# A diffusion-transformer block with a routed MLP on one core: queries turned by VectorE and exchanged through DRAM, in another order of steps

## The chip, the core and the metric

The kernel runs on one core of one Trainium2 chip. The metric is the device time of one execution in microseconds (us), the median of three runs. All operands that matter here are float32, and all sizes below are per execution.

## What is computed

The reference, cut to the part around the change (16 sequences of 256 tokens, width 256, 16 heads of 64):

```python
shift = jax.nn.silu(t) @ W_ada.T + b_ada
h = _ln(x, ln1_g, ln1_b) + shift
qkv = (h @ Wqkv.T).reshape(b, n, 3, H, HD)
q = _ln(qkv[:, :, 0].transpose(0, 2, 1, 3), qn_g, qn_b)   # per head, over its 64 values
k = _ln(qkv[:, :, 1].transpose(0, 2, 1, 3), kn_g, kn_b)
v = qkv[:, :, 2].transpose(0, 2, 1, 3)
scores = jnp.einsum('bhnd,bhmd->bhnm', q, k) / jnp.sqrt(jnp.float32(HD))
attn = jax.nn.softmax(scores, axis=-1)
o = jnp.einsum('bhnm,bhmd->bhnd', attn, v)
x = x + o.transpose(0, 2, 1, 3).reshape(b, n, H * HD) @ Wout.T
```

Behind it come a gate over 8 experts, the choice of the 512 best tokens of each expert, a norm, a two-layer MLP per expert (256 to 1024 to 256, GELU) on the chosen tokens, and an addition of the weighted results to the tokens.

## The kernel before

The kernel has two phases. The first does, sequence by sequence, the norm, the projections to queries, keys and values, the attention, the output projection and the gate logits. The second chooses tokens and runs the experts, in 16 jobs (8 experts, two halves of their tokens); the change touches it only in the buffers of a few small tiles.

**One sequence in the first phase.** `First` normalises 256 tokens and turns them on TensorE (L646). `Group` (L671) stands for 512 of the 3072 projected columns and 128 tokens: there are twelve in a sequence, with g = 0, 1 for queries, 2, 3 for keys, 4, 5 for values, and t = 0, 1 for the two halves of the tokens. Each runs two matmuls of 128x512 (L683). Query and key groups are then squared on ScalarE (L696), summed per head on VectorE (L700), raised to -0.5 on GpSimd (L103) and scaled on VectorE (L716). A head's 64 values now lie along the free dimension and have to lie along the partitions.

**Two ways to turn them.** Queries go through TensorE: four transposes of 128x128 (L725), and ScalarE reads the result from PSUM, applies the gain and bias of the norm and writes it to `qT` (`evict`, L737). Keys of sequences 1 to 14 go another way. VectorE transposes them in blocks of 32x32 (`turn`, L749). When both halves of a group pair are done, SP writes the 512 KB to a DRAM tile (`away`, L756, one DMA) and reads them back with the blocks in their places (`back`, L764, four DMAs of 32 partitions and 128 KB each). ScalarE then applies gain and bias in place (`affine`, L770). The attention probabilities take the same way: VectorE turns them (`turn`, L832), SP writes them away (L840) and brings them back (L854), eight times a sequence. One write with its four reads is called an exchange below. Sequences 0 and 15 (`DIRECT`) use no exchange at all.

**Attention.** `Quad` handles four heads, in two steps of two: scores (L794), maxima on VectorE (L802), exponentials with sums on ScalarE (L811), reciprocal on VectorE (L818), normalising on GpSimd (L822), the turn and its exchange, and the product with the values (L881). `Tail` is the output projection (L907), the residual (L914), a second norm, two stores of 128 KB, and the gate logits (L944).

**What sets the order.** Nothing is scheduled at run time. Each step is entered in a `Plan` with an engine, a duration and the buffers it uses, and a table `PLACES` holds one number for each step. The program is the steps sorted by that number (L1497), and each engine runs its instructions in that order. The steps of several sequences are thus interleaved by hand. All DMAs of the first phase stand on SP's queue in this order too; an SP instruction that waits holds up all behind it. Buffers are rings: three 512 KB tiles `pb` hold what VectorE turned, keys and probabilities alike; four DRAM tiles `blocks`; four tiles `prT` for what came back; two of `qT`, `kT`. The entries in the plan for an exchange read

```python
at(q + 10, "SP", 0.36, partial(a.away, i), [pb], [(1, blocks)], [pb, blocks], lag=1.0)
at(q + 11, "DMA", 1.6, nothing, [(1, blocks)], [blocks], [pb], lag=1.7)
at(q + 14, "SP", 1.6, partial(a.back, i), [blocks], [(1, prT)], [blocks, prT], lag=0.0)
at(q + 15, "DMA", 2.6, nothing, [(1, prT)], [prT], [blocks], lag=1.7)
```

so that the plan gives the transfers of an exchange 1.6 + 2.6. The "DMA" steps issue nothing. Loads of `x` and the stores of `Tail` have no "DMA" step.

Of the kernel before, what the change touches and what calls it, by code (L numbers as in the profile page):

```python
# [9 lines left out]
F32 = mybir.dt.float32  # L10
I32 = mybir.dt.int32
BF16 = mybir.dt.bfloat16
AF = mybir.ActivationFunctionType
# [5 lines left out]
P = 128  # L19
B, N, D = 16, 256, 256  # L20
# [44 lines left out]
def kernel(  # L65
# [83 lines left out]
    def make_others():  # L149
# [33 lines left out]
        0, 0, 3.3, 4.54, 3.75, 5.04, 4.42, 7.33, 0.23, 0, 8, 9.39, 18.02, 16.03, 11.2, 13.11,  # L183
        23.2, 20.01, 0, 0, 0, 0, 0, 0, 0, 4.02, 4.97, 5.83, 3.5, 4.21, 6.16, 6.67, 7.33, 10.88,
        12.83, 14.5, 15.29, 17.42, 23.39, 24.13, 14.6, 16.55, 19.41, 20.2, 22.6, 25.38, 26.05,
        12.61, 14.56, 15.43, 17.17, 22, 22.79, 23.46, 18.21, 20.16, 21.4, 22.19, 24.59, 25.83,
        26.72, 29.9, 32.28, 31.78, 34.69, 26.28, 28.23, 28.97, 30.46, 32.44, 39.3, 40.4, 33.51,
        35.46, 36.17, 37.06, 39.25, 44.82, 45.92, 35.24, 37.19, 37.9, 38.94, 41.05, 47.16, 47.98,
        40.04, 42.03, 42.74, 43.53, 45.51, 49.93, 50.64, 42.21, 46.59, 48.2, 50.15, 28.01, 30.17,
        31.32, 33.31, 36.97, 37.69, 29.57, 30.36, 34.22, 41.77, 43.49, 33.04, 45.27, 29.03, 31.7,  # L190
        32.77, 35.24, 44.38, 45.43, 30.77, 33.73, 36.15, 43.94, 44.94, 34.97, 46.29, 47.38, 37.41,
        38.65, 39.44, 46.32, 56.74, 58.42, 41.65, 42.53, 45.41, 58.91, 60.37, 43.77, 63.58, 38.43,
        39.85, 41.07, 47.23, 62.1, 62.91, 40.45, 43.98, 48.14, 62.69, 63.4, 45.22, 64.6, 67.15,
        53.84, 55.37, 58.91, 60.42, 69.53, 70.25, 56.57, 57.46, 61.33, 72.14, 72.9, 60.15, 78.82,
        61.08, 62.32, 63.89, 66.36, 71.7, 72.41, 62.92, 64.85, 67.27, 72.58, 73.39, 66.09, 79.84,
        80.93, 76.93, 82.47, 83.26, 84.77, 90.28, 91.04, 78.53, 79.32, 85.68, 93.62, 97.65, 84.5,
        98.81, 77.95, 80.33, 84.22, 87.6, 89.84, 90.55, 79.13, 85.18, 86.69, 94.06, 96.49, 86.42,
        97.79, 100.1, 113.62, 117.31, 119.21, 119.11, 120.6, 121.31, 132.34, 133.24, 134.29,
        135.07, 124.06, 129.13, 130.78, 130.28, 131.14, 131.65, 134.74, 135.18, 136.69, 137.38, 0,
        25.19, 25.9, 27.27, 12.59, 13.3, 15.1, 47.76, 48.65, 50.38, 52.33, 53.04, 53.83, 55.97,  # L200
        63.13, 65.81, 54.86, 56.96, 57.67, 58.46, 60.44, 61.64, 52.11, 54.06, 54.77, 55.71, 58.27,
        65.47, 66.48, 57.18, 59.87, 61.04, 62.24, 64.22, 65.01, 65.81, 67.17, 70.47, 72.07, 76.37,
        59.35, 61.3, 69.97, 71.92, 66.07, 68.02, 68.73, 69.52, 71.5, 74.75, 75.47, 67.8, 69.75,
        70.46, 71.4, 73.38, 74.17, 73.02, 74.97, 75.68, 76.47, 79.73, 81.3, 82.47, 75.2, 77.22,
        77.93, 78.72, 80.93, 81.86, 82.66, 84.02, 87.32, 88.92, 93.22, 81.75, 86.64, 88.11, 90.06,
        85.21, 86.59, 87.38, 92.27, 93.76, 87.79, 88.84, 93.18, 94.37, 90.08, 95.17, 96.53, 99.83,
        101.43, 108.83, 90.72, 91.96, 94.57, 98.56, 100.76, 93.16, 95.53, 97.65, 100.15, 96.77,
        101.56, 104.03, 107.33, 109.11, 117.09, 119.02, 96.77, 99.55, 100.59, 103.75, 105.35,
        98.35, 99.14, 102.84, 104.14, 102.57, 106.15, 107.51, 110.95, 117.51, 127.68, 99.68,
        101.97, 103.18, 107.74, 109.6, 101.37, 102.22, 106.83, 108.99, 106.56, 110.59, 114.31,  # L210
        117.61, 121.71, 128.7, 132.26, 103.03, 105.96, 106.99, 111.44, 112.79, 104.75, 105.54,
        110.53, 112.18, 108.53, 113.59, 115.91, 119.71, 124.31, 139.03, 105.93, 107.33, 108.12,
        112.35, 115.81, 107.93, 109.58, 113.26, 114.6, 112.01, 116.61, 120.11, 123.41, 126.91,
        140.05, 143.4, 110.87, 113.4, 114.33, 118.2, 119.82, 114, 115.29, 117.29, 119.21, 117.02,
        128.61, 132.71, 136.01, 141.21, 147.73, 109.85, 111.41, 117.1, 121.61, 123.7, 115.21,
        118.06, 120.7, 124.31, 120.43, 125.11, 131.11, 134.41, 137.01, 146.71, 148.82, 161.94,
        165.79, 166.94, 166.94, 167.8, 171.31, 179.5, 180.6, 181.82, 182.8, 173.1, 177.15, 180.31,
        179.07, 180.05, 180.81, 181.6, 182.35, 184, 184.96, 0, 25.71, 26.66, 27.6, 28.45, 29.7,
        31.37, 80.71, 81.52, 83.48, 86.14, 87.19, 88.51, 90.49, 94.5, 96.98, 86.23, 88.34, 89.05,
        90.39, 92.56, 95.58, 91.74, 94.07, 94.98, 95.77, 97.75, 100.7, 101.55, 94.95, 98.14,  # L220
        98.95, 99.74, 102.74, 103.53, 104.33, 105.69, 108.99, 111.71, 116.25, 104.05, 106.5,
        111.74, 113.84, 101.3, 104.14, 106.73, 108.65, 110.81, 118.11, 119.51, 106.95, 109.08,
        110.21, 114.17, 116.42, 118.31, 120.44, 122.39, 123.1, 124.4, 126.72, 129.57, 130.64,
        118.71, 120.66, 121.37, 122.52, 124.92, 127.32, 128.12, 129.51, 132.81, 134.41, 138.71,
        130.61, 132.75, 140.92, 143.89, 123.19, 125.52, 126.31, 131.95, 133.42, 126.12, 127.27,
        131.04, 132.81, 130.13, 137.61, 139.61, 142.91, 145.41, 159.19, 122.17, 127.93, 128.72,
        133.77, 136.77, 128.53, 129.68, 132.86, 136.16, 130.92, 141.31, 143.81, 147.11, 149.61,
        158.17, 161.1, 137.14, 138.47, 139.56, 142.34, 143.4, 139.07, 140.52, 143.25, 144.79,
        142.07, 145.59, 148.01, 151.31, 153.81, 172.23, 138.16, 140.27, 141.48, 144.89, 147.11,
        140.87, 142.44, 145.8, 148.32, 144.62, 149.12, 152.21, 155.51, 158.01, 171.21, 175.48,  # L230
        148.6, 149.84, 150.63, 153.77, 154.83, 150.44, 152.26, 154.68, 155.74, 153.5, 157.11,
        160.61, 169.71, 172.31, 188.93, 149.62, 151.64, 153.71, 159.02, 160.19, 152.24, 154.67,
        159.93, 162, 156.95, 162.8, 164.81, 168.11, 169.71, 187.91, 190.02, 157.3, 158.39, 159.18,
        162.88, 163.96, 158.99, 160.14, 163.79, 165.18, 162.61, 165.98, 167.34, 182.91, 185.51,
        196.77, 156.28, 159.59, 161.59, 165.61, 168.74, 161.4, 162.55, 164.7, 168.13, 163.79,
        171.81, 174.91, 178.21, 179.81, 197.79, 198.88, 207.36, 211.52, 212.87, 212.67, 213.53,
        214.04, 227.17, 227.9, 229.12, 230.2, 218.67, 222.51, 224.16, 224.13, 224.99, 229.46,
        226.8, 228.2, 231.3, 232.08, 0, 26.23, 27.42, 48.75, 27.93, 28.94, 48.42, 130.17, 131.31,
        132.56, 134.51, 135.23, 136.26, 139.67, 144.53, 145.25, 134.96, 136.91, 137.87, 138.66,
        141.47, 144.01, 142.8, 144.75, 145.46, 146.71, 148.93, 150.49, 151.59, 144.98, 146.93,  # L240
        147.72, 148.59, 151.04, 152.84, 153.64, 156.41, 159.71, 162.21, 166.75, 151.09, 153.22,
        160.06, 163.51, 152.82, 155.63, 156.35, 157.14, 160.8, 165.41, 166.08, 154.55, 156.5,
        157.21, 160.84, 162.82, 164.57, 167.59, 169.54, 170.25, 171.04, 173.85, 176.72, 177.39,
        165.86, 170.04, 172.05, 172.92, 174.97, 175.76, 176.61, 177.97, 181.31, 182.91, 187.21,
        179.87, 181.86, 184.45, 186.4, 170.34, 171.45, 172.6, 175.07, 176.37, 172.65, 173.56,
        175.98, 178.15, 174.8, 184.51, 188.11, 191.41, 194.37, 205.47, 169.32, 170.85, 171.64,
        178.16, 181.58, 173.25, 174.52, 177.25, 182.19, 176.98, 189.81, 191.17, 194.47, 196.97,
        204.45, 206.56, 177.61, 179.45, 180.9, 183.23, 184.35, 178.85, 179.64, 184.14, 185.29,
        182.96, 190.17, 192.77, 198.88, 201.17, 215.91, 178.63, 180.98, 183.61, 189.36, 194.7,
        180.38, 182.65, 186.57, 195.31, 185.12, 196.11, 199.57, 202.87, 205.37, 214.89, 217,  # L250
        189.8, 191.04, 193.89, 199.56, 201.54, 191.64, 192.43, 196.77, 200.32, 195.92, 202.34,
        207.97, 211.27, 213.77, 235.21, 194.88, 196.12, 196.91, 206.32, 207.38, 197.92, 202.57,
        207.23, 208.59, 203.81, 209.39, 212.17, 215.47, 217.07, 236.23, 237.32, 195.9, 198.52,
        201.11, 202.62, 217.22, 199.12, 200.15, 203.53, 216.61, 202.35, 218.02, 219.67, 226.26,
# [1361 lines left out]
```

## Time and profile before

| what | value |
|---|---|
| median of three runs | 1104.54 us (1104.27 to 1107.28) |
| the profiled execution | 1106.04 us, of which its span is 1104.2 us |
| granted TensorE clock, mean | 0.99 |
| exchange phase, first write of keys to last read of probabilities | 69.0 to 761.8 us |
| output projections, first to last matmul | 117.1 to 818.0 us |
| busy, whole span: PE, DVE, ACT, POOL | 1070.6, 778.9, 596.1, 616.2 us |
| DMA of SP's queue (q1) | 139520 packets, 197.71 MB |

PE is TensorE, PEld its weight loads, DVE is VectorE, ACT ScalarE, POOL GpSimd, SP the engine that issues DMAs. The profile's views used below are: the page with its busy shares and its 40 slices; the groups of instructions by line, with their busy time, mean duration of one and what ended the idle time before them; the timeline; the waits; and tables of windows, which give for a stretch of time (us from the start of the span) each engine's busy time, the granted clock, the mean busy share of the 16 DMA engines (packets that overlap are counted double, so it can exceed 1) and the GB/s moved.

### The profile page before, as it was taken

How to read it: one execution, taken by the hardware profiler on the slowest of the kernel's cores; microseconds unless marked ns; L12 is line 12 of the kernel's file. 1: busy time of each engine (PE TensorE's matmuls, PEld its weight loads, DVE VectorE, ACT ScalarE, POOL GpSimd, SP SyncE). 2: the span in 40 equal slices, each digit the busy share in tenths (PEclk: the TensorE clock that was granted, in tenths of full speed). 3: DMA queues.
4: the chain of work that ended last, by engine and by line, in shares of the span. 5: the costliest groups of instructions: out<-in, count | busy, mean ns of one | idle time of the engine just before them, and what ended most of it. 6: DMA issues, size and time to landing. Idle time of an engine off the chain costs nothing. (4 is left out here: it accounts for less than half of the span.)

```text
span 1104.2 us, 18872 instructions
## 1 busy us (share of the span) xinstructions
PE 1070.6 (97%) x5835; PEld 714.8 (65%) x5835; DVE 778.9 (71%) x2201; ACT 596.1 (54%) x1656; POOL 616.2 (56%) x997
## 2 busy tenths in 40 slices
PE   7999999999999999999899999999988999999996
PEld 4555656566565655656465655656767888888885
DVE  6657888777778777786678787676568488654540
ACT  2768666565766566566557667576522333322331
POOL 3766776776676665675657666565411233333332
PEclk9999999999999999999999999999999999999998
DMA  6013998785888787796787778895130456555661
GB/s 211 1 39 123 277 259 237 230 255 166 248 260 227 226 246 234 201 260 211 211 251 227 228 224 240 243 256 179 63 102 20 113 189 200 170 162 175 196 201 19
DMA packets 147539, 209.20 MB, mean 189 GB/s; under 512 B 15088, under 2 KB 122864, under 8 KB 147440
## 3 DMA queue, kind: packets, MB, share of 16 engines
q1 hardware_dynamic: 139520, 197.71, 60.0%
q0 software_dynamic: 6144, 8.39, 4.1%
q10 hardware_dynamic: 1776, 1.90, 0.5%
q8 instruction: 47, 0.77, 0.3%
q14 instruction: 52, 0.43, 0.1%
HBM read 121.96 MB, written 85.98 MB: 188 GB/s over the span
## 5 line engine op out<-in xcount | busy, mean ns | idle before, releaser
L683 PE MATMUL pm<-wq,hT 128*128 128x512 f32 x768 | 360.4, 605 | 5.0 <-DVE qk L716 2.8
L822 POOL TENSOR_SCALAR pr<-pr,sums 128x256 f32<-128x256 f32 x512 | 237.1, 481 | 112.2 <-DVE sums L818 92.9
L811 ACT ACTIVATE pr<-sc,nmax 128x256 f32<-128x256 f32 x512 | 238.0, 480 | 97.5 <-DVE nmax L802 80.3
L683 PEld LDWEIGHTS pm<-wq,hT 128*128 128x128 f32 x768 | 137.3, 192 | 146.1 <-issue 131.1
L103 POOL TENSOR_TENSOR ss<-ss,neghalf 128x8 f32<-128x8 f32 x128 | 210.5, 1645 | 10.6
L802 DVE TENSOR_REDUCE nmax<-sc 128x2 f32<-128x512 f32 x256 | 165.3, 676 | 16.9 <-PE sc L794 16.3
L832 DVE STREAM_TRANSPOSE pb<-pr 128x512 f32<-128x512 f32 x224 | 149.9, 690 | 18.5 <-POOL pr L822 13.6
L794 PE MATMUL sc<-kT,qT 64*128 64x256 f32 x1024 | 135.4, 397 | 0.0
L881 PE MATMUL po<-prT,v 128*64 128x256 f32 x1024 | 127.6, 388 | 1.1 <-DVE gates L950 1.1
L700 DVE TENSOR_REDUCE ss<-sq 128x8 f32<-128x512 f32 x128 | 86.0, 672 | 47.3 <-ACT sq L696 46.8
L794 PEld LDWEIGHTS sc<-kT,qT 64*128 64x128 f32 x1024 | 92.8, 188 | 40.8 <-issue 25.4
L696 ACT ACTIVATE sq<-pm 128x512 f32<-128x512 f32 x128 | 76.9, 603 | 77.3 <-PE pm L683 75.9
L1301 POOL DMA_INDIRECT out<-y,idx x32 | 51.2, 1601 | 119.8 <-DVE y L1295 66.9
L1268 PE MATMUL ph<-xT,w 128*128 128x256 f32 x512 | 117.6, 383 | 0.0
L907 PE MATMUL pw<-wo,oT 128*128 128x256 f32 x512 | 116.6, 381 | 0.3 <-DVE qk L716 0.3
L1284 PE MATMUL py<-w,hid 128*128 128x256 f32 x512 | 116.3, 380 | 0.0
L716 DVE TENSOR_TENSOR qk<-pm,ss 128x512 f32<-128x512 f32 x128 | 87.0, 681 | 36.9 <-POOL ss L103 35.9
L907 PEld LDWEIGHTS pw<-wo,oT 128*128 128x128 f32 x512 | 96.0, 190 | 23.2 <-issue 9.4
L811 ACT ACTIVATION_READ_ACCUMULATOR pr<-sc,nmax 128x1 f32 x512 | 107.6, 210 | 0.0
L881 PEld LDWEIGHTS po<-prT,v 128*64 128x64 f32 x1024 | 67.1, 137 | 61.5 <-issue 21.1
L1275 ACT ACTIVATE hid<-ph,vec 128x256 f32<-128x256 f32 x128 | 60.4, 474 | 84.2 <-PE ph L1268 76.3
L1284 PEld LDWEIGHTS py<-w,hid 128*128 128x128 f32 x512 | 95.6, 190 | 12.8
(140 smaller groups left out, 1132.6 us busy)
## 6 DMA issues: line engine op xcount, KB each, us to landing
blocks<-pb SPq DMA_DIRECT2D x112, 512.0 KB
prT<-blocks SPq DMA_DIRECT2D x448, 128.0 KB
w<-in_fc2T SPq DMA_DIRECT2D x16, 1024.0 KB
w<-in_fc1T SPq DMA_DIRECT2D x16, 1024.0 KB
kblocks<-kb SPq DMA_DIRECT2D x28, 512.0 KB
kT<-kblocks SPq DMA_DIRECT2D x112, 128.0 KB
out<-tok SPq DMA_DIRECT2D x32, 128.0 KB
xn_dram<-tn SPq DMA_DIRECT2D x32, 128.0 KB
```

The costliest lines, as they stand in the source:

```text
L103: nc.gpsimd.tensor_tensor(dst, src, neghalf[:, : src.shape[1]], ALU.pow)
L683: nc.tensor.matmul(self.pm, hTs[self.b][:, c, bass.ts(self.t, P)], wq[:, c, bass.ts(self.g, GW)], start=(c == 0), stop=(c == DC - 1),)
L716: engine.tensor_tensor(self.qk.rearrange("p (h d) -> p h d", d=HD), src.rearrange("p (h d) -> p h d", d=HD), self.ss[:, 1, :].unsqueeze(2) ...
L794: nc.tensor.matmul(self.sc[i, j][:, t, :], qTs[self.b][rows, hp, bass.ts(t, P)], keys[rows, hp] if direct else keys[rows, hp // 4, hp % 4] ...
L802: nc.vector.tensor_reduce(self.nmax[i, j], self.sc[i, j], AX.X, ALU.max, negate=True)
L811: nc.scalar.activation(self.pr[i, j][:, t, :], self.sc[i, j][:, t, :], AF.Exp, bias=self.nmax[i, j][:, t : t + 1], scale=1.0, accum_out=se ...
L822: nc.gpsimd.tensor_scalar(self.pr[i, j][:, t, :], self.pr[i, j][:, t, :], self.sums[i][:, 1, j, t : t + 1], 1.0, ALU.mult, ALU.mult,)
L832: nc.vector.transpose(self.pb[i][:, :, :, j].rearrange("p k c t n -> p t k c n"), self.pr[i, j].rearrange("p t (k c m) -> p t k c m", c=TB ...
L881: nc.tensor.matmul(self.po[j * HD : (j + 1) * HD, i, :], vs[self.b][:, c, bass.ts(4 * self.d + 2 * i + j, HD)], prT[:, j, c] if self.b in ...
L907: nc.tensor.matmul(self.pw, oTs[self.b][:, hp // 2, self.t, hp % 2, :], wo[:, hp, :], start=(hp == 0), stop=(hp == HP - 1),)
L1268: nc.tensor.matmul(self.ph[f], self.w1[:, c, bass.ts(f, P)], self.xT[:, c, :], start=(c == 0), stop=(c == DC - 1),)
L1284: nc.tensor.matmul(self.py[i], self.hid[:, f, bass.ts(i, P)], self.w2[:, f, :], start=(f == 0), stop=(f == FC - 1),)
```

## The change

Queries of sequences 1 to 14 take the keys' way: `turn` on VectorE, one write and four reads through DRAM, then gain and bias on ScalarE from a tile `qraw` (two buffers) into `qT`, in two instructions of 128x512. The four TensorE transposes and the reading of PSUM of those groups go. Routing's tiles for masks, places and choices lie in the `pb` ring in place of tiles of their own. The plan's durations of an exchange become 1.2 + 2.0 with longer lags, and all of `PLACES` is new (3863 numbers in place of 3779). In it the last output projection, which has the place 800.67 before, has the place 777.79.

```diff
             def back(self):
-                kT = self.keys()[:, self.g - 2].rearrange("p k t h m -> p k (t h m)")
+                if self.g < 2:
+                    self.raw = work.tile([P, QB, TB, HP // 2, SQ], F32, tag="qraw", bufs=2, name="qraw")
+                else:
+                    self.raw = self.keys()[:, self.g - 2]
+                raw = self.raw.rearrange("p k t h m -> p k (t h m)")
                 for q in range(QB):
                     nc.sync.dma_start(
-                        kT[bass.ts(q, SQ)], self.blocks[:, :, q].rearrange("k d n -> d k n")
+                        raw[bass.ts(q, SQ)], self.blocks[:, :, q].rearrange("k d n -> d k n")
                     )
             def affine(self):
+                if self.g < 2:
+                    qT = of_sequence(qTs, self.b, "qT", [P, HP, N])
+                    for t in range(TB):
+                        nc.scalar.activation(
+                            qT[:, 4 * self.g : 4 * self.g + 4, bass.ts(t, P)].rearrange(
+                                "p h (k m) -> p k h m", m=SQ
+                            ),
+                            self.raw[:, :, t], AF.Identity, bias=qgb[:, 1:2], scale=qgb[:, 0:1],
+                        )
+                    return
...
-                self.mask = route.tile([P, 2, 2 * P], F32, tag="mask", name="mask")
+                both = work.tile([P, 4, 2 * P], F32, tag="pb", bufs=3, name="both")
+                self.mask, self.place_ = both[:, :2], both[:, 2:]
...
-                self.places = route.tile([P, 2 * P], F32, tag="places", name="places")
+                three = work.tile([P, 3, 2 * P], F32, tag="pb", bufs=3, name="three")
+                self.places, one, self.chosen = (three[:, k] for k in range(3))
...
-                    if g > 1 and b not in DIRECT:
+                    if b not in DIRECT:
...
-                            at(p + 7, "DMA", 1.6, nothing, [(1, blocks)], [blocks], [kb], lag=1.7)
+                            at(p + 7, "DMA", 1.2, nothing, [(1, blocks)], [blocks], [kb], lag=2.0)
...
-                            at(p + 11, "DMA", 2.6, nothing, [(1, "kT", b, g)], [(2, "kT", b, g)], [blocks], lag=1.7)
+                            at(p + 11, "DMA", 2.0, nothing, [(1, to, g)], [(2, to, g)], [blocks, to], lag=2.2)
+                            if g < 2:
+                                at(p + 15, "ACT", 1.0, a.affine, [(2, to, g)], [("qT", b, g)], [to, ("qT", b)], lag=0.22)
+                            else:
+                                at(p + 15, "ACT", 0.85, a.affine, [(2, to, g)], [("kT", b, g - 2)], [to], lag=0.22)
```

## The prediction

> **What bounds the kernel now.** I read the page first, for which engine is full and when.
>
> ```profile
> PE 1070.6 (97%) x5835; PEld 714.8 (65%) x5835; DVE 778.9 (71%) x2201; ACT 596.1 (54%) x1656; POOL 616.2 (56%) x997
> ...
> DMA  6013998785888787796787778895130456555661
> ```
>
> TensorE is busy nearly throughout. A slice is 27.6 us, and in those of the exchange phase (69.0 to 761.8 us) the DMA engines are mostly at 7 to 9 tenths, second to PE alone. Since a busy PE need not be PE at its peak, the timeline decides whether its instructions really touch.
>
> ```profile
> 325.12 0.66 PE L646 MATMUL ph<-ident,xn 128*128 128x128 f32 x4
> 325.61 0.60 PE L725 MATMUL pq<-ident,qk 128*128 128x128 f32 x4
> 326.05 1.88 PE L683 MATMUL pm<-wq,hT 128*128 128x512 f32 x4
> ```
>
> Each group starts before the modelled end of the one ahead, so PE is the bound. Four transposes of queries hold it from 325.61 to 326.05, 0.44 us; at 315.21 and at 340.11 the same four hold it 0.53 us. Next, the windows: per stretch each engine's busy us, the clock, the DMA share and GB/s.
>
> ```profile
> 66.00:100.00 34.00, 34.00 (x170) 19.26 (x168) 20.38 (x37) 26.43 (x70) 20.80 (x31) 1.00 0.21 72
> 100.00:765.00 665.00, 658.57 (x3321) 389.54 (x3321) 517.48 (x1036) 424.19 (x1253) 452.63 (x784) 1.00 0.81 233
> ...
> 480.00:490.00 10.00, 10.00 (x53) 4.93 (x54) 6.91 (x14) 6.70 (x15) 7.23 (x10) 1.00 1.01 294
> 640.00:650.00 10.00, 10.00 (x50) 5.33 (x51) 8.05 (x13) 3.60 (x6) 9.39 (x15) 1.00 1.02 257
> ```
>
> From 100 to 765 us PE idles 6.4 us, DVE 148, ACT 241; the DMA engines move 233 GB/s at a share of 0.81. What they move when nothing is left idle: ten stretches of 10 us have a share of 1.00 or more, and they moved 266, 287, 284, 281, 270, 294, 257, 280, 287 and 269 GB/s, 277.5 in the mean. Of the 27 stretches of 25 us from 100 to 775 only two moved over 260 GB/s (277 and 282). Last, the groups of instructions and SP's waits.
>
> ```profile
> L737 ACT ACTIVATE qT<-pq,qgb 128x512 f32<-128x512 f32 x64 | 49.9, 784 | 28.2 <-PE pq L725 27.9
> L749 DVE STREAM_TRANSPOSE kb<-qk 128x512 f32<-128x512 f32 x56 | 39.0, 697 | 0.5
> L770 ACT ACTIVATE kT<-kT,vec 128x1024 f32<-128x1024 f32 x28 | 34.9, 1248 | 2.6 <-DMA kT<-kblocks 2.5
> ```
>
> ```profile
> SPq L840 <- DVE pb L832: 67.0, 33, 8.2
> SPq L756 <- DVE kb L749: 52.2, 19, 12.2
> SPq L854 <- DMA blocks<-pb: 42.9, 19, 4.2
> ...
> SPq L764 <- DMA kblocks<-kb: 20.2, 9, 3.6
> ```
>
> The keys' way is priced by its own rows. SP often waits for VectorE to supply a tile (the DMA has slack today), and for 63.1 us (42.9 + 20.2) it waits until a write has landed before it may issue the reads, 0.45 us for each of 140 exchanges.
>
> **The change, part by part.**
>
> *TensorE.* 14 sequences x 4 query groups = 56 groups lose their four transposes: 56 x 0.49 us (between 0.44 and 0.53) = 27.4 us less, all on the path that bounds today. The built program agrees: its `pq` transposes fall from 288 to 64.
>
> *ScalarE.* 56 x 784 ns go, 56 instructions of 128x512 from `qraw` come. No row has this form. Half of a key's 1248 ns gives 624 ns, the PSUM row 784; so 0 to 9 us less, on an engine with 241 us idle. I take 0. What matters is the added wait: 28 times ACT now stands until query reads have landed. Behind it in ACT's order are exponentials and squares; VectorE's sums and GpSimd wait for those, and PE for the PSUM they release. Today's 28 such waits cost 2.6 us in all; if a read were late by a whole exchange (3.8 us, below) each time, 28 would cost 106 us. That upper end is the DMA case itself and is not added to it.
>
> *VectorE.* 56 more turns x 697 ns = 39.0 us, of 148 us idle in the phase. Hidden at 556 of 665 us, but it leaves less room to catch up after a wait; uncovered, it is 39.0 us.
>
> *SP.* 28 writes and 112 reads more. A write's issue takes 0.34 us, a read's 0.43 (medians of L756, L764): 57.7 us of issue. SP spent 119.2 us of the run waiting for VectorE at the two lines above, so this is covered; but queries' writes and reads now stand in one order with the probabilities' reads and the stores, and hold those up when they wait.
>
> *DMA.* An exchange moves 2 x 524 KB = 1.049 MB, at 277.5 GB/s 3.78 us; 28 more are 29.4 MB. Before 100 us lie two of them (sequence 1's), when the share is 0.21 and they cost nothing. From 100 us on there are today 233 GB/s x 665 us = 155 MB; with 26 exchanges more, 182.2 MB. At 277.5 GB/s that is **657 us without a gap, against 665 us today and 638 us (665 - 27) that TensorE would need.** This is the disputed term. Its bounds are the extremes of the ten full stretches: 294 GB/s gives 620 us (TensorE binds), 257 gives 709. I take the mean, and add gaps: SP's landing waits at 0.45 us for 166 exchanges are 75 us, and during most of them other transfers still run; with a quarter, 19 us, the phase takes 676 us, which is a sustained 270 GB/s.
>
> *The order.* `PLACES` moves nearly every instruction on all queues, and I can't price it line by line. It puts the last output projection 22.9 us earlier, nearly what TensorE loses; but it allots 3.2 us to the transfers of an exchange and nothing to the loads of x and the stores (0.79 MB a sequence, 2.8 us at 277.5 GB/s), where this trace gives 3.78. An order is not a time: if transfers come later than its places assume, in-order engines wait. The old order allotted 4.2 us, more than a transfer takes, and PE had no gaps.
>
> *Routing's tiles.* The last turn into `pb` is written away at 753.8 us; routing's masks come after the last output projections (818.0). The ring is idle for 64 us, so sharing it costs nothing; without that cover it would be one exchange's wait, 3.8 us, once.
>
> [...] The trace's full stretches move 257 to 294 GB/s. [...]
>
> **Sum.** Phase 676 - 665 = +11 us; before and behind it nothing changes (no exchange runs there). 1106.04 us (the profiled run: span 1104.2 and 1.8 around it) + 11 = 1117; the runs' median lies 1.5 us below that execution, so I write 1116.
>
> **The rivals.**
>
> 1. *Transfers become the bound (my forecast), 1116 us.* For it: the demand after, 182.2 MB in 665 us = 274 GB/s, is what today's time would need, more than 25 of 27 stretches moved. Against: those stretches were not starved for want of speed but of demand. From 257 GB/s (+44, 1148) to 277.5 without a gap (-8, 1096).
> 2. *TensorE stays the bound, faster: 1077 us* (1104.5 - 27). One mechanism: transposes leave PE's full queue and the transfers keep up. It decides from 182.2 MB / 638 us = 286 GB/s on; three of the ten full stretches (287, 294, 287) reach it. For it: PE has no gaps today although the share already reaches 1 in ten stretches, so the buffers do cover bursts of that kind. Against: the mean of 277.5, and any gap.
> 3. *Small waits spread over all engines, 1136 us.* When PE does wait, it also loses clock: from 530 to 540 us it was busy 7.49 us and the granted clock was 0.83, so 2.5 + 1.7 = 4.2 us in one event, the only deep one in the phase. Once per sequence, 14 x 4.2 = 59, less the 27, is +32 us. It needs `prT` or `qT` to land some 2 us behind its place.
>
> That the change doesn't do what it says is excluded by the count of transposes.
>
> **How the numbers follow.** Transfers bound: 0.70, of which 0.52 slower, 0.10 within 0.3% (between about 272 and 276 GB/s sustained), 0.08 faster. TensorE bound: 0.20, faster. Waits and clock: 0.10, of which 0.07 slower, 0.01 the same, 0.02 faster. So faster 0.30, same 0.11, slower 0.59, where 0.3% (3.3 us) is about what a measurement of this kernel can tell from no change. The range reaches from 1080 (leaving out the full gain of rival 2) to 1142 (leaving out a rate under 259 GB/s): some 1 in 10 lies beyond each end.
>
> **What would show it.** Right: q1 carries about 20,000 packets more (28 x 720); the DMA line stands at 9 through the exchange phase, with 265 to 275 GB/s from 100 us on; SP waits less for `pb` and `kb` of VectorE and more for landed writes; PE shows idle time before L881, L794 or L683 that it does not have now; ACT's new query line waits for DMA. The transposes of L725 fall to 64, the reads of PSUM (L737) from 72 to 16, VectorE's turns of `kb` rise to 112. Wrong: PE stays without gaps in the phase and the share passes 0.9 at 285 GB/s or more; then rival 2 holds, and my rate was that of bursts and not of the engines. Idle PE while the DMA share is still 0.8 would speak for rival 3.

## The result and the profile after

The changed kernel takes 1099.1 us in the median (1096.4 to 1102.8, 20 runs), the kernel before, run beside it, 1104.5 us (20 runs; one of them, at 6162 us, stands apart from all the others). The ratio is 0.9952 (95% interval 0.9942 to 0.9962): 5.4 us faster, where 12 slower were forecast. The profiled span fell from 1104.2 to 1096.8 us.

The page of the profile after, its busy shares, its DMA and GB/s lines in 40 slices of 27.4 us, and SP's queue:

```profile
PE 1050.9 (96%) x5611; PEld 685.9 (63%) x5611; DVE 809.8 (74%) x2257; ACT 591.5 (54%) x1656; POOL 615.8 (56%) x997
...
DMA  6026989999998999998999999986120456565661
GB/s 213 1 77 188 273 261 294 285 281 261 282 278 269 282 280 284 283 286 255 281 294 275 285 283 266 310 265 186 64 101 20 132 172 202 169 174 171 194 202 19
...
q1 hardware_dynamic: 159680, 227.08, 70.2%
```

The DMA engines now stand at 8 or 9 tenths from the fifth slice to the 27th, and q1 has 20,160 packets more. Windows of after say what that means for TensorE (columns as in the prediction):

```profile
100.00:765.00 665.00, 648.98 (x3146) 369.35 (x3146) 548.02 (x1095) 424.73 (x1267) 452.56 (x785) 1.00 0.96 275
125.00:725.00 600.00, 583.98 (x2808) 328.91 (x2806) 498.18 (x995) 382.93 (x1136) 408.33 (x708) 1.00 0.98 281
```

From 100 to 765 us PE now idles 16.0 us instead of 6.4, and the DMA share went from 0.81 to 0.96. Undisturbed by the ramps at both ends, the kernel holds 281 GB/s for 600 us. The idle time stands before the projections and the scores; the page's lines for these two, before and after (the last numbers are the idle time in us and what ended most of it):

```profile
L683 PE MATMUL pm<-wq,hT 128*128 128x512 f32 x768 | 360.4, 605 | 5.0 <-DVE qk L716 2.8
L794 PE MATMUL sc<-kT,qT 64*128 64x256 f32 x1024 | 135.4, 397 | 0.0
```

```profile
L688 PE MATMUL pm<-wq,hT 128*128 128x512 f32 x768 | 361.5, 606 | 13.1 <-DVE qk L721 6.3
L813 PE MATMUL sc<-kT,qT 64*128 64x256 f32 x1024 | 137.4, 396 | 3.5 <-ACT kT L789 3.0
```

The groups of after (by form) show the new work, SP's waits and all engines' waits show who stands still:

```profile
L754 DVE STREAM_TRANSPOSE kb<-qk 128x512 f32<-128x512 f32 x112 | 77.6, 697 | 6.5 <-DMA blocks<-pb 5.6
L781 ACT ACTIVATE qT<-qraw,qgb 128x512 f32<-128x512 f32 x56 | 42.8, 819 | 12.0 <-DMA qraw<-kblocks 11.7 <-issue 0.2
L789 ACT ACTIVATE kT<-kT,vec 128x1024 f32<-128x1024 f32 x28 | 34.8, 1245 | 18.9 <-DMA kT<-kblocks 18.4 <-issue 0.3
L730 PE MATMUL pq<-ident,qk 128*128 128x128 f32 x64 | 9.2, 278 | 0.8 <-DVE qk L721 0.7
```

```profile
SPq L761 <- DVE kb L754: 90.4, 20, 56.6
SPq L873 <- DMA blocks<-pb: 68.6, 45, 5.3
...
SPq L773 <- DMA kblocks<-kb: 28.0, 20, 3.3
SPq L859 <- DVE pb L851: 22.4, 20, 4.6
```

```profile
DVE pb L851 <- DMA kblocks<-kb: 9.5, 9, 2.0
DVE kb L754 <- DMA blocks<-pb: 5.6, 6, 1.8
...
DVE pb L851 <- DMA blocks<-pb: 2.5, 4, 1.1
```

ScalarE waits 30.1 us (11.7 + 18.4) for tiles that come back, where it waited 2.5. VectorE, which waited 4.3 us (3.7 + 0.6) at its turns until a write had left a ring tile free, waits 17.6 there, in these three lines. SP's wait for VectorE at the probabilities' write fell from 67.0 to 22.4 us, and its waits for landed writes rose from 63.1 to 96.6 (68.6 + 28.0). The 90.4 us at the keys' and queries' write hold one wait of 56.6 us ahead of the first exchange, which before stands in another line of SP's waits:

```profile
SPq L756 <- DVE sums L818: 69.4, 7, 57.6
```

Without that one wait SP stands 33.8 us for a turned tile there, where before it stood 52.2. So the transfers are late where they were not.

How much of the time that is, one instruction tells: the residual addition of the output projection, whose first and last starts enclose the whole attention. The views of that one line, before and after:

```profile
L914 DVE TENSOR_TENSOR tok<-pw,xs x32: 384/424/426, 120.7 to 818.6; 128x256 f32<-128x256 f32 x32
```

```profile
L933 DVE TENSOR_TENSOR tok<-pw,xs x32: 385/424/427, 121.7 to 809.4; 128x256 f32<-128x256 f32 x32
```

The attention shrank from 697.9 to 687.7 us, by 10.2. It begins 1.0 us later, and what follows its last residual is 287.4 us long instead of 285.6. -10.2 + 1.0 + 1.8 = -7.4 us, the difference of the spans. So of the 27.4 us that TensorE was to save, 10.2 arrived.

### The profile page after: what moved, and what is told of

Same layout as the page of the kernel before. It is cut to its first block, busy times and chain, and to the rows that moved or that the text cites. A ratio compares the mean times of both kernels' runs of the same rounds, so it can differ in the third digit from the quotient of the medians.

```text
span 1096.8 us, 18716 instructions
## 1 busy us (share of the span) xinstructions
PE 1050.9 (96%) x5611; PEld 685.9 (63%) x5611; DVE 809.8 (74%) x2257; ACT 591.5 (54%) x1656; POOL 615.8 (56%) x997
## 5 line engine op out<-in xcount | busy, mean ns | idle before, releaser
L688 PE MATMUL pm<-wq,hT 128*128 128x512 f32 x768 | 361.5, 606 | 13.1 <-DVE qk L721 6.3
L1286 PEld LDWEIGHTS ph<-xT,w 128*128 128x128 f32 x512 | 95.4, 190 | 12.8
```

The source lines that it names most:

```text
L688: nc.tensor.matmul(self.pm, hTs[self.b][:, c, bass.ts(self.t, P)], wq[:, c, bass.ts(self.g, GW)], start=(c == 0), stop=(c == DC - 1),)
L1286: nc.tensor.matmul(self.ph[f], self.w1[:, c, bass.ts(f, P)], self.xT[:, c, :], start=(c == 0), stop=(c == DC - 1),)
```

## The experiments

The theory (T): TensorE does save its 27 us, and transfers take back some 16 of them. The rival (W): waits that come with the new places and the new dependences take it back, whatever the transfers' rate. All ratios are against the kernel before, run on the same chip; in brackets stand the 95% intervals. Placement of steps that a kernel here adds is mine, by the rule stated with it. Where two changed kernels are compared, the difference in us is one of medians that can come from different chips; by the ratios it comes out up to 1 us larger or smaller (e4's 15.6 us below would be 16.6, e14's 13.0 would be 14.0).

### What the transfers cost, and what TensorE saves

**e4** is the changed kernel without the queries' 28 writes and 112 reads. VectorE still turns, ScalarE still applies gain and bias, but straight from the turned tile, so the blocks are left in the wrong places.

```diff
             def away(self, kb):
+                if self.g < 2:
+                    self.raw = kb[0]
+                    return
...
             def back(self):
                 if self.g < 2:
-                    self.raw = work.tile([P, QB, TB, HP // 2, SQ], F32, tag="qraw", bufs=2, name="qraw")
+                    return
...
-                                at(p + 15, "ACT", 1.0, a.affine, ...)
+                                more.append((PLACES[len(plan.steps) - 4] + 0.1, a.affine))
```

> The changed kernel without the queries' 56 writes... that is 28 writes and 112 reads: gain and bias are applied straight to the tile that VectorE turned, at the place where the write stood, so the blocks stay in the wrong places. VectorE, ScalarE and TensorE do all they do in the changed kernel. Theory T: the 27 us come free, 1075 to 1084 us. Rival W (waits in the order, VectorE's 39 us more): 1092 to 1100.

1083.5 us, 0.9802 [0.9789, 0.9814]. One window and the residual line of e4:

```profile
100.00:765.00 665.00, 661.26 (x3264) 383.39 (x3262) 554.10 (x1114) 436.52 (x1288) 459.40 (x796) 1.00 0.82 237
```

```profile
L935 DVE TENSOR_TENSOR tok<-pw,xs x32: 378/424/425, 123.0 to 793.6; 128x256 f32<-128x256 f32 x32
```

With the share back at 0.82, PE idles 3.7 us, and the attention takes 670.6 us, 27.3 less than before. That is TensorE's term (27.4) nearly to the tenth; 2.7 us of it are idle time that before still had, so the transposes themselves were worth some 25. The transfers with their issue and waits (and the later place of gain and bias that they ask for) cost 1099.1 - 1083.5 = 15.6 us. This lies in T's range.

### The order without the exchange, the exchange without the order

**e1** and **e3** keep the new places and put queries back on TensorE, all or one half: the transposes stand where the turn stood, the reading of PSUM 0.9 behind.

```diff
+        through = lambda b, g: False      # e1;  e3: g == 0
...
+                    if b not in DIRECT and g < 2 and not through(b, g):
+                        when = PLACES[len(plan.steps)]
+                        at(p + 5, "PE", 0.45, a.transposes)
+                        more.append((when + 0.9, a.evict))
...
```

> The new order of steps alone: queries of all sequences go through TensorE as before, their transposes standing where the new kernel has the turns on VectorE, their reading from PSUM 0.9 places later. Theory T (in the changed kernel the transfers are the bound): with the queries' 29.4 MB gone TensorE binds again and has its 27 us of transposes back, 1104 us, between 1100 and 1108. Rival W (the new order brings waits of in-order engines, whatever is transferred): 27 us of transposes on top of 1099, less what overlaps, 1112 to 1126.

> The new order with half of the change: only the first query group pair (heads 0 to 7) is exchanged, the second goes through TensorE. Theory T: 155 MB + 13 exchanges x 1.049 = 168.6 MB need 600 us at 281 GB/s, TensorE needs 665 - 13.7 = 651, so TensorE binds and nearly all of 13.7 us is gained: 1091 us, between 1087 and 1096. Rival W: half of a gain and half of its waits, 1100 to 1103.

e1: 1126.6 us, 1.019 [1.0177, 1.0203], 21 us slower than before on the same chip and at the upper end of W's range, far from T's. Its residual line:

```profile
L933 DVE TENSOR_TENSOR tok<-pw,xs x32: 384/425/426, 129.1 to 837.1; 128x256 f32<-128x256 f32 x32
```

The attention starts 8.4 us later than before and takes 10.1 longer (PE idles 14.0 us from 100 to 765). So the new places, with my placing of the transposes in them, are no gain by themselves. This is W's mechanism, but in the kernel without the exchange. How much belongs to the order and how much to my placing in it stays open.

e3: 1102.2 us, 0.9969 [0.996, 0.9979]. T had expected it below the changed kernel and was wrong; it lies in W's range: 28 groups of transposes are back on TensorE (13.7 us at 0.49), PE still idles 7.9 us, and 14 exchanges spared do not make up for it.

**e2** is the reverse: before's places with the exchange, the write 1, the reads 5 and gain and bias 10 behind the turn, from tiles of their own, one buffer each.

```diff
-                    if g > 1 and b not in DIRECT:
+                    if b not in DIRECT and g < 2 and through(b, g):
+                        when = PLACES[len(plan.steps)]
+                        at(p + 5, "DVE", 0.61, partial(a.turn, turned[g]))
...
+                        if t:
+                            more.append((when + 1.0, partial(a.away, turned[g])))
+                            more.append((when + 5.0, a.back))
+                            more.append((when + 10.0, a.affine))
```

> The exchange alone: the old order of steps, with the queries' turns where their TensorE transposes stood, the write 1, the reads 5 and the gain and bias 10 places behind the second turn, a 512 KB tile of their own for the turned queries and one buffer for what comes back. Theory T: the same bytes at the same rate, so the time of the changed kernel within some us, 1095 to 1106. Rival W (the order decides): the old order has no room for the exchange, PE waits for queries and the time is 1110 to 1135.

1167.5 us, 1.0557 [1.0533, 1.058], beyond both ranges. A window and a wait of e2:

```profile
100.00:765.00 665.00, 607.63 (x2819) 345.34 (x2819) 501.85 (x1005) 386.48 (x1144) 415.00 (x717) 0.97 0.88 252
```

```profile
ACT qT L776 <- DMA qraw<-kblocks: 54.4, 24, 6.6
```

PE idles 57 us and loses clock too (0.97), while the DMA share is only 0.88: ScalarE stands 54.4 us for queries that had not landed at the place where I had put gain and bias, with exponentials queued behind it. The same exchange in the new places is 68 us faster. So the exchange put into the old places in this way loses far more than it can gain. Whether the old places could carry it with gain and bias further behind the turn, or with a second `qraw`, was not tried; that an order made for the exchange is a condition of the change is likely, but not shown.

### Is it the bytes?

**e5** and **e6** add 28 writes of 512 KB from SBUF to DRAM that nobody reads, to before and to after, one behind each key write (14.7 MB; 52 us at 281 GB/s).

```diff
+        def spare(k):
+            put = dram.tile([P, 1024], F32, name=f"spare{k}")
+            nc.sync.dma_start(put, wq[:, 0, :1024])
```

> The kernel before, with 28 more writes of 512 KB (14.7 MB) to DRAM tiles that nobody reads, one behind each write of keys. Theory T (here the transfers have slack): 155 + 14.7 = 169.7 MB at 281 GB/s need 604 us of the phase's 665, so TensorE hides them: 0 to 8 us more, 1104 to 1113. Rival W (in-order waits, not the rate): SP's order is held up alike before and after the change, so about the same small cost in both, 2 to 10 us.

> The changed kernel with the same 28 writes. Theory T (the transfers bind): each byte now costs, 14.7 MB at 281 GB/s are 52 us; at most a quarter of it fits into what is left idle, so 35 to 55 us more, 1134 to 1154. Rival W: 2 to 10 us more, 1101 to 1109.

e5: 1113.5 us, 1.0073 [1.0058, 1.0089], 8 us, in the range of both theories. e6: 1119.1 us, 1.0124 [1.0106, 1.0142], 20 us above the changed kernel. T had expected 35 to 55, W 2 to 10; it lies between the two. The window of e6:

```profile
125.00:725.00 600.00, 574.28 (x2724) 324.28 (x2723) 486.31 (x974) 369.05 (x1090) 399.66 (x690) 0.99 1.00 292
```

The rate rose from 281 to 292 GB/s, although the share had already stood at 0.98. A single rate for all bytes is too simple: the added writes found room that the mix before did not seem to have.

**e10** and **e15** move tiles of 512 KB (one stretch: 1 MB) alone; nothing is computed, `x` is copied to the output.

```diff
+    exchanges(60, N, 2)                    # write, then four reads, two ahead
+    exchanges(30, 2 * N, 2)                # the same with rows of 2 KB
+    exchanges(60, N, 2, reads=False)       # writes alone
+    exchanges(60, N, 4, writes=False)      # reads alone
```

> No block is computed here: tokens are copied to the output, then four stretches of transfers run one behind the other with nothing else on the chip: 60 exchanges as in the kernel, 30 of twice the size (rows of 2 KB in place of 1 KB read back), 60 writes alone, 60 times four reads alone, always two exchanges ahead. If the engines' rate is what limits the changed kernel, the first stretch moves about what it does there (281 GB/s), 270 to 295; if the other engines' traffic slows the transfers, it moves over 310.

Windows of e10 in the order of the diff (columns: DVE, POOL, clock, share, GB/s):

```profile
60.00:240.00 180.00, 0.00 (x0) 0.00 (x0) 1.00 1.05 334
260.00:400.00 140.00, 0.00 (x0) 0.00 (x0) 1.00 1.03 399
405.00:470.00 65.00, 0.00 (x0) 0.00 (x0) 1.00 1.03 416
490.00:610.00 120.00, 0.00 (x0) 0.00 (x0) 1.00 1.03 230
```

Reads into 32 partitions run at 230 GB/s, writes from 128 at 416. One after the other, an exchange would run at 296 (2.28 us + 1.26 us for 1.049 MB); together they reach 334, so they overlap in part. Reads and writes differ here in more than direction: a read is 128 KB in rows of 1 KB, a write 512 KB in rows of 4 KB. How much each of these does was not taken apart, but with twice the row and twice the transfer the exchange moves 399 GB/s. Since 281 in the kernel is less, e15 tries other shapes of the queue: the four reads in the order of partition quarters 0, 2, 1, 3; exchanges in lumps of two; one write ahead instead of two; and reads alone in the order 0, 2, 1, 3.

> No block is computed: tokens are copied to the output, then four stretches of transfers alone on the chip. 60 exchanges two ahead with the quarters in the order 0, 2, 1, 3; 60 in lumps of two writes and two times four reads; 60 only one ahead; 60 times four reads alone in the order 0, 2, 1, 3. Beside the 339 GB/s of 60 exchanges in plain order and 229 of reads alone: if the halves of the partitions matter, the first stretch moves over 350 and the last over 260. If the order of a queue alone can bring 339 down to the changed kernel's 281, the lumps or the shorter lead move 300 or less; if not, the other engines' work does it.

```profile
52.00:235.00 183.00, 0.00 (x0) 0.00 (x0) 1.00 0.99 327
240.00:430.00 190.00, 0.00 (x0) 0.00 (x0) 1.00 1.06 318
430.00:620.00 190.00, 0.00 (x0) 0.00 (x0) 1.00 1.03 313
640.00:760.00 120.00, 0.00 (x0) 0.00 (x0) 1.00 1.11 259
```

None comes down to 281, so none of these forms of the queue explains the kernel's rate. But reads alone go from 230 to 259 with the other order of quarters.

### Reads in another order of quarters

**e14** is the changed kernel, **e17** the kernel before, with that order in both `back`s.

```diff
-                for q in range(QB):
+                for q in (0, 2, 1, 3):
```

> The changed kernel with the four reads of each exchange in another order: partitions 0-31, 64-95, 32-63, 96-127 in place of 0-31, 32-63, 64-95, 96-127. If what holds the reads down is that 32 neighbouring partitions at a time take them (reads alone moved 229 GB/s, writes of 128 partitions 415), neighbours in the queue now go to different halves, overlap better, and transfers bind less: 1085 to 1095 us. If the rate is set by packets of 1 KB, no difference: 1097 to 1102.

> The kernel before with the four reads of each exchange in the order 0, 2, 1, 3. If the 13 us that this order saves in the changed kernel come from transfers that bind there, it saves little here, where TensorE binds: 1101 to 1106 us. If the order of quarters helps in some other way (SP, landing of single tiles), it saves a like amount here: 1088 to 1096.

e14: 1086.1 us, 0.9825 [0.981, 0.984], 13 us below the changed kernel. A window and two waits of e14:

```profile
100.00:765.00 665.00, 660.04 (x3246) 381.47 (x3243) 555.00 (x1110) 433.43 (x1286) 458.00 (x796) 1.00 0.89 278
```

```profile
ACT kT L789 <- DMA kT<-kblocks: 6.9, 9, 1.3
ACT qT L781 <- DMA qraw<-kblocks: 3.6, 3, 1.7
```

The same transfers now fit beside TensorE: PE idles 5.0 us instead of 16.0, ScalarE waits 10.5 us instead of 30.1, and the time is 2.6 us above e4, which has no query transfers at all. e17: 1105.5 us, 1.0006 [0.9996, 1.0015]: no gain. Its window:

```profile
100.00:765.00 665.00, 658.86 (x3320) 389.38 (x3317) 518.42 (x1037) 423.57 (x1255) 451.79 (x783) 1.00 0.75 233
```

The DMA share fell here too (0.81 to 0.75, at the same 233 GB/s), but TensorE binds: PE idles 6.1 us, where it idled 6.4. That the same edit is worth 13 us after and nothing before is the plainest sign that the bound had moved to the transfers, and within them to the reads. Visiting the halves of the partitions in turn gained 13% alone (259 over 230 GB/s) and 13 us in the kernel. That the halves are the cause is not shown: for that case e15's expectation named over 260 GB/s for the reads alone and over 350 for the exchange, and 259 and 327 came.

### Waits, buffers and the number of exchanges

**e12** issues every `back` 1.5 places later, so that SP should stand less in front of unlanded writes; **e9** has four ring tiles for turned data instead of three, and one `qraw`.

```diff
+            place + 1.5 * (getattr(run, "func", run).__name__ == "back")      # e12
...
-tag="pb", bufs=3        # e9: four times
+tag="pb", bufs=4
-tag="qraw", bufs=2
+tag="qraw", bufs=1
```

> The changed kernel with every group of four reads 1.5 places later in SP's order, behind more of the other transfers, so that SP waits less for landed writes. The prediction's term (SP's landing waits leave the DMA engines idle, 19 us): 1082 to 1094. Against it (other transfers run meanwhile, the engines idle 2% of the phase): no gain, 1097 to 1106, later if returned tiles now come late.

> The changed kernel with four tiles in the ring of turned blocks instead of three (and one buffer for returned queries instead of two, to make room). Theory T: same bytes, same rate, 1096 to 1102 us. Rival B (buffers: VectorE stood 17.6 us for a free tile of this ring, and that is what delays TensorE): 1085 to 1093 us.

e12: 1095.9 us, 0.9917 [0.9897, 0.9937]; e9: 1096.2 us, 0.9921 [0.9908, 0.9935]: some 3 us each, e9 at the lower end of T's range and e12 between its two. Why these gain 3 us is not shown. In e12 SP's landing waits stayed at 97.0 us (96.6 in after), so it did not take away what it was made to take away.

**e8** puts 5 of the 28 query exchanges back on TensorE (g = 1 of every third sequence), by e1's edit; **e11** is e8 with e9's four tiles, and **e16** adds the quarters' order of e14.

```diff
+        through = lambda b, g: not (g == 1 and b % 3 == 2)
```

> The changed kernel with 5 of its 28 query exchanges taken back (second pair of groups in sequences 2, 5, 8, 11 and 14, through TensorE). Theory T: 5.2 MB less are 18.7 us of transfers, more than the 15.6 us that they cost over the kernel without transfers (1083.5); TensorE gets 4.9 us back and some waits of these groups as with half of them: 1088 to 1095 us, faster than both kernels. Rival W: taking back 14 gave 1102, so taking back 5 gives 1099 to 1101.

> Five of 28 query exchanges taken back and four tiles in the ring of turned blocks. If transfers and the ring each cost something in the changed kernel, the two gains (6.3 and 2.9 us) add up in part: 1088 to 1092 us. If the ring only mattered because transfers were late, nothing is added to the 1092.8 of the five alone: 1092 to 1094.

> Five of 28 query exchanges taken back, four tiles in the ring, and the quarters in the order 0, 2, 1, 3. If the order of quarters speeds the reads: under 1090, at best 1083 + 5 = 1088 us. If not, as without it, 1090 to 1093.

e8: 1092.8 us, 0.9887 [0.9872, 0.9902], 6.3 below the changed kernel, although TensorE has 5 x 2 groups of transposes more, 4.9 us: with 23 exchanges the share is 0.93 and PE idles 7.3 us. That is T's range, where e3 came out in W's: 14 exchanges taken back cost 2 to 3 us, 5 taken back gain 6 to 7. My places for the returned steps stand in both, and how the two fit together stays open. e11: 1091.8 us, 0.9884 [0.9866, 0.9903], no more than e8. e16: 1085.5 us, 0.9827 [0.981, 0.9845], not to be told from e14. Once the reads are quick enough, sparing some brings nothing. e14 and e16 beat both kernels of this case; e14 is the simpler.

### Routing's tiles

**e13** is the kernel before with that part of the change alone.

```diff
-                self.mask = route.tile([P, 2, 2 * P], F32, tag="mask", name="mask")
+                both = work.tile([P, 4, 2 * P], F32, tag="pb", bufs=3, name="both")
+                self.mask, self.place_ = both[:, :2], both[:, 2:]
```

> The kernel before with the new home of routing's tiles and nothing else of the change. All theories: no difference, within 2 us of the kernel before.

1105.4 us, 0.9996 [0.9985, 1.0006]: nothing.

## Why the prediction was wrong

**The mechanism held, its size did not.** The transfers did move up beside TensorE, and of the signs foretold most came: 20,000 packets, 9 tenths in the DMA line, SP's wait for `pb` down (for `kb` too, but for the one wait ahead of the first exchange) and those for landed writes up, ScalarE's new line waiting for DMA, 64, 16 and 112 instructions. PE's new idle time stands before the projections (13.1 us instead of 5.0) and the scores (3.5 instead of 0.0); before the product PE waits 1.8 us for tiles read back. The rate of 275 GB/s from 100 us on is the upper end of the foretold 265 to 275. But the price of the transfers over what TensorE needs was 38 us in the forecast (676 - 638) and 15.6 us on the chip, and with it the sign turned.

**The step that failed is the DMA term, and in it "with a quarter, 19 us, the phase takes 676 us, which is a sustained 270 GB/s".** The bytes were near: from 100 to 765 us after moved 275 GB/s x 665 us = 183 MB (182.2 foretold). The rate was not. The phase took about 655 us (665 - 10.2), so the 182.2 MB moved at a sustained 278 GB/s; over the 600 us between the ramps it was 281, with every wait in it, and that is 3.5 above the mean that the forecast took as the rate without a gap. So the 19 us for gaps, laid on top of that mean, had nothing to stand for. Without them the same sum gives the 657 us and the 1096 us that the first rival names as its other end, 3 below the measured 1099.1. That this comes so near is partly luck, since it still goes by one rate for all bytes (below) and leaves out 2.8 us at the two ends.

SP's landing waits themselves rose, to 0.575 us per exchange (96.6 / 168), and in e14 SP still stood 65.8 us for landed writes (49.0 + 16.8) while PE idled 5.0 us. SP waiting for a write to land is not an engine without work; transfers issued earlier run meanwhile: in the two longest such waits of after (338.9 to 344.2 and 505.8 to 510.3 us) the DMA engines moved 274 and 211 GB/s at shares of 0.92 and 0.81. The share of 0.98 would not show this by itself, because packets that overlap count double and the exchange alone stands at 1.05 (e10). What rate the kernel would reach without any such wait is not shown: e12 was to test that and did not, since its waits stayed.

**One rate for all bytes was the wrong measure, too.** Reads and writes differ by 416 to 230 GB/s when alone (e10), 14.7 MB of spare writes cost 20 us instead of 52 (e6), and an order of quarters that moves the same bytes took 13 of the 15.6 us away (e14). The ten full stretches were full by the share, which counts the time of packets: the share is 1.03 at 230 GB/s and at 416. So a share of 1 did not say that the rate was the highest to be had.

**TensorE's 27.4 us** were right (27.3 in e4 by the residuals, with the 2.7 us of idle time named there). Leaving TensorE paid where it binds, by 5.4 us in the changed kernel and by some 19 in e14 (by its ratio).

**ScalarE** took 819 ns for 128x512, above both ends of my bound (624 and 784): 56 x 35 ns = 2.0 us more than the PSUM reads that went. It idles 240 us of the phase, so nothing came of it. Its waits of 30.1 us are part of the transfers' price, far from the 106 us of the upper end.

**The order** was left unpriced, and it can weigh more than any term that was priced: e2, with the exchange in the old places as I put it there, lies 68 us above the changed kernel, outside my range. My forecast of 1116 assumed neither such a loss nor its cure. Nor did I price the start (+1.0 us) and the part behind the last residual (+1.8): "before and behind it nothing changes" was wrong by 2.8 us. e13, 285.8 us there, shows that it is not the sharing of tiles; e1 and e4 have the same 287.4 and 287.3, so it seems to come with the places. These are single profiles (e17, with before's places, has 284.7), and which step does it stays open.

**The rivals.** Small waits and clock: in after the granted clock is 1.00 from 100 to 765 us, although PE idles 16.0 us there; that rival came true in e2 alone (57 us idle, a clock of 0.97). TensorE stays bound: its deciding rate was 286 GB/s; after has 281 and misses it by 5, and e14 (287 from 125 to 725 us) has PE nearly without gaps. That agrees with the line drawn, but does not test it: once TensorE binds, the rate is no more than what TensorE's pace asks for (233 GB/s in before and in e17, at shares of 0.81 and 0.75).

**What stays open** is why the kernel holds 281 GB/s where the exchange alone holds 313 to 334 in every form tried with rows of 1 KB: the loads of `x` and the stores between, or the engines' own traffic, were not taken apart. No run separates a higher rate of the reads from their earlier landing. Nor is shown *why* the order of quarters helps in the kernel by more than alone, where the mixed exchange did not gain from it (327 against 334).

## What to carry to other kernels

Price a transfer by its own form (direction, size, rows, the partitions it fills), not by its bytes alone (here 230 GB/s for the reads and 416 for the writes), and test the bound by leaving the transfers out before giving the engines a rate. A queue that waits for a landed write says nothing yet of idle DMA engines: read the share and the GB/s of the same window (here 274 GB/s in the longest such wait). Where narrow reads bind, the order in which they visit the partitions is a free edit to try (here 13 us in the changed kernel, nothing in the one before), and when transfers are added to a fixed order of steps, look at which engine then stands waiting for them (in e2 ScalarE, 54.4 us).

## What the runs showed of the hardware

- Reads of 128 KB into 32 partitions, in rows of 1 KB: 230 GB/s alone; writes of 512 KB from 128 partitions: 416. With rows of 2 KB and DMAs of twice the size the exchange moves 399 instead of 334 (e10).
- Visiting the partition quarters in the order 0, 2, 1, 3 instead of 0, 1, 2, 3: reads alone 259 instead of 230 GB/s (e15); the kernel 1086.1 instead of 1099.1 us (e14).
- The DMA share is no measure of the rate: 1.03 with 230 and with 416 GB/s (e10); 0.81 and 0.75 with the same 233 (before and e17).
